# A seven-product scheme for A11 B11 of two row-block pairs, chained in PSUM, in an fp32 relational graph layer

## The chip, the core and the metric

The kernel runs on one NeuronCore of a Trainium2 chip. TensorE (PE) multiplies into PSUM, which has eight banks of 128 partitions x 512 fp32 values; VectorE (DVE) and ScalarE (ACT) read and write PSUM and SBUF; GpSimd (POOL) issues the indirect gathers and scatters; SyncE (SP) issues plain DMAs. Each engine works through its own queue in order, and semaphores tie the queues together. The metric is the device time of one execution in microseconds (us).

## What is computed

Everything is fp32. There are 1250 nodes with 1024 features, 20000 edges and 8 edge types.

```
h = max(layernorm(x), 0)
u = h @ root + bias
for r in range(8):
    mask = (edge_type == r)
    sums = segment_sum(h[src] * mask, dst);  cnt = segment_sum(mask, dst)
    u = u + (sums / max(cnt, 1)) @ weight[r]
z = concat([u, h], 1) @ w_gate + b_gate
out = x + tanh(u) * z + h * (1 - z)
```

The kernel multiplies first and gathers afterwards: it forms h @ weight[r] for every type, h @ root and h @ (lower half of w_gate), ten products of 1250 x 1024 by 1024 x 1024 (matrices s = 0 to 9), gathers rows of them per edge, and ends with u @ (upper half of w_gate).

## The kernel before

**Tiling.** The 1250 rows are ten blocks of 128. Blocks d and d+5 form row-block i = 0 to 4, so each matrix s is five calls of `product`, i = 0 to 4. In a call the left side is a 2 x 2 arrangement of 128 x 512 parts and the right side one of 512 x 512 quarters. `product` computes it with seven products instead of eight (Winograd's form of Strassen): of A11, A12, A22 and sums S1 to S4 on the left, with quarters and sums t1 to t4 on the right. I call such a product a *large* one: `add` (L354) issues four matmuls with a moving operand of 512 columns. Three of the sums live in one PSUM bank `b`: A11, then S2 and then S3 and A22 are added onto it, and between two additions ACT copies the running value out (L395, L402, L380, L429). So each addition to `b` must wait until ACT has read the one before it.

**Inner products.** For s > 0 the rows i = 0, 1 and i = 2, 3 are pairs. The product of A12 with b21 of both rows of a pair is itself done with seven *small* products (class `Second`): `add` (L212) issues two matmuls with 256 columns each. For s > EARLY = 3, that is matrices 4 to 9, the product of S4 with b22 is done so too (class `Third`, its sums in `room`). The small products are put between large ones by hand: `product` calls `filled("first")`, `"fifth"`, `"sixth"`, `"third"`, `"seventh"` and `"fourth"` after the large product of that number, and `step` has a table `fill` of what goes there. `q` is the pair's `Third`, `e` its `Second`. After each large product (and after a fill that returns true) `done()` calls `beside(j)` with j = 0, 1, 2 and so on; there DVE forms the sums, and `between(j)` issues the *slots*: one gather on POOL (L1168) and one DVE multiply-add of 128 x 1024 (L1173) per slot, 1.19 to 1.24 per call for s = 5 to 9.

**The order in matrices 4 to 9** is, by row: i = 0: A11, S1, S2, `e.second`, S3, `q.second`, A22. i = 1: A11, `e.first` (2 small), `q.first` (3), S1, `e.sixth` (2), S2, `e.seventh`, S3, `e.fourth`, `q.last` (3), A22. i = 2: A11, S1, S2, `e.first`, S3, `e.sixth`, `q.second`, `e.seventh`, A22, `e.fourth`. i = 3: A11, `q.first`, S1, S2, `e.second`, S3, `q.last`, A22. i = 4 is alone: A11, S1, S2, S4, S3, A12, A22.

**PSUM.** `bank()` (L121) hands out six banks named `ps`; `ps_n` holds S1 of the first row of a pair until the second (`hold`, L279), `ps_q` is one bank of `Third`. Each `product` takes two of the six for `b` and `c`.

**The end.** After matrix 9, five more calls of `product` multiply u by the upper half of w_gate. In each, `gate_u` transposes two blocks of the next u on PE (`transposed`, L315: four banks, read out alternately by ACT and DVE) after the S4 product, and `gate_rows`, `gate_load` and `finish` put gathers on POOL and elementwise work on DVE.

Of the kernel before, what the change touches and what calls it, by code (L numbers as in the profile page):

```python
# [19 lines left out]
def tile_rgcn_highway(  # L20
# [98 lines left out]
    node_dram = [dram.tile([KEYS, 1], I32, name=f"node_dram{g}") for g in range(G)]  # L119

    def bank():  # L121
        return psum.tile([P, 512], F32, name="ps", bufs=6)


    wbuf = [wpool.tile([P, KQ, Q], F32, name=f"w{i}") for i in range(9)]
# [57 lines left out]
    class Second:  # L183
# [52 lines left out]
        def second(self):  # L236
            self.a = bank()[:, :H]
            self.add(self.a, self.a12, self.b21, True)
# [15 lines left out]
    class Third:  # L254
# [53 lines left out]
        def last_to(self, to, to1, c):  # L308
# [3 lines left out]
                                 to1.rearrange("p (a n) -> p a n", a=2),  # L312
                                 self.b[:, None, :].to_broadcast([P, 2, H]))

    def transposed(aop, part, of, n, relu=False):  # L315


        for half, to in enumerate(((A11, A12), (A21, A22))[part]):
            p = bank().rearrange("p (k f) -> p k f", k=KQ)
            for i in range(KQ):  # L320
                k = KQ * half + i
                nc.tensor.transpose(p[:, i, :n], of[:n, k * P:(k + 1) * P], ident[:n, :n])  # L322
            to_n, p_n = aop[:, to, :, :n], p[:, :, :n]
            if half and relu:
                nc.vector.tensor_scalar_max(to_n, p_n, 0.0)
            elif half:
                nc.vector.tensor_copy(to_n, p_n)
            else:
                nc.scalar.activation(to_n, p_n, AF.Relu if relu else AF.Copy)
            if n < P:  # L330
                nc.gpsimd.memset(aop[:, to, :, n:], 0.0)
# [7 lines left out]
                                                                     aop[:, b])  # L339

    def product(aop, w, to, between=lambda j: None, last=None, pieces=1, whole=True,
                fill=None, second=None, third=None, inner=None):

        c11, c12 = to[0][:, :Q], to[0][:, Q:]  # L350
        c21, c22 = to[1][:, :Q], to[1][:, Q:]
        step = [0]

        def add(b, i, fresh=False, at=slice(0, Q)):  # L354
            for k in range(KQ):
                nc.tensor.matmul(b[:, at], aop[:, i, k, :], w.of[i][:, k, at],  # L356
                                 start=(fresh and k == 0), stop=(k == KQ - 1),
                                 skip_group_check=True)

        def done():  # L360
            between(step[0])
            step[0] += 1

        def filled(name):
            if fill and name in fill and fill[name]():
                done()

        def p3():
            add(c, S4)
            if third:  # L370
                third(c)
            else:
                nc.vector.tensor_add(c12, c12, c)  # L373
            done()
            filled("third")

        def p7():
            d = rows.tile([P, Q], F32, name="part", bufs=2)
            add(b, S3)
            nc.scalar.copy(d, b)  # L380
            nc.vector.tensor_add(c22, c22, d)  # L381
            done()
            filled("seventh")
            return d

        def p2():
            a = bank()
            add(a, A12, True)
            nc.vector.tensor_add(c11, c11, a)
            done()  # L390

        b = bank()
        c = inner.hold() if inner and inner.holds else bank()
        add(b, A11, True)
        nc.scalar.copy(c11, b)  # L395
        done()
        filled("first")
        if second:
            second()
            p2()  # L400
        add(c, S1, True)
        nc.scalar.copy(c22, c)  # L402
        done()
        filled("fifth")
        add(b, S2)
        nc.scalar.copy(c12, b)  # L406
        done()
        filled("sixth")
        if whole and not third:
            p3()  # L410
            d = p7()
            if not second:
                p2()
        else:
            d = p7()
            if third:
                last(d, 0)
            if inner:
                inner.then(c)
                done()  # L420
                filled("third")
            else:
                p3()
        if pieces == 1:
            add(b, A22)
            if last:
                last(b, 0)
            else:
                nc.scalar.copy(c21, b)  # L429
        else:  # L430
            for j in reversed(range(pieces)):
                at = slice(j * Q // pieces, (j + 1) * Q // pieces)
                b = bank()
                add(b, A22, True, at)
                last(b[:, at], at.start, d[:, at])
        done()
        filled("fourth")
# [12 lines left out]
    def thirds(s):  # L450

        return s > EARLY

    waiting, waiting_third = {}, {}

    def step(s, i, between=lambda j: None, second=None):

# [20 lines left out]
            nc.sync.dma_start(to, t[:n])  # L478

        def beside(j):  # L480
            new = fac[s + 1]
            if i == 0 and j == 0 and s > 0:
                fac[s].make_t4()
            if two and i == 0:
                sums(j)
            if q and i % 2 == 0 and j == 1:
                q.sums()
            if q and i % 2 and j == 1:
                q.next_sums()
                q.first_to(to[:, Q:])  # L490
            if q and i % 2 and j == 4:
                q.fifth_to(t[0][:, Q:])
            if two and (i, j) == (1, 6):
                Second(fac[s], 2).left()
            if (s, i, j) == (0, 0, 3) or (s > 0 and (i, j) == (3, 0)):
                new.load_first()
            if (s, i, j) == (0, 0, 3) or (s > 0 and (i, j) == (3, 2)):
                new.load_next()
            if i == NP - 1:
                if j == 0:  # L500
                    new.load_b22()
                elif j == 1:
                    new.make_t1()
                elif j == 3:
                    new.load_b21()
                elif j == 4:
                    new.make_t2()
                elif j == 5:
                    new.make_t3()
            between(j)  # L510

        def sums(j):
# [5 lines left out]
            if j == (0 if s > EARLY else 4):  # L518
                e.left()

        fill = {}
        q = None
        if two:
            e, to = waiting[i - i % 2]
            if thirds(s):
                if i % 2 == 0:
                    waiting_third[i] = Third(fac[s], i, room)
                q = waiting_third[i - i % 2]
                q.holds = i % 2 == 0

                def then(c):
                    if q.holds:
                        q.second(c)
                    else:
                        q.last(c)
                        q.last_to(to[:, Q:], t[0][:, Q:], c)
                        put(i - 1, 0, to)

                q.then = then
            if i == 0:  # L540
                fill = dict(sixth=lambda: (e.second(), e.second_to_first(to)))
            elif i == 1:
                fill = dict(first=lambda: (e.first(), q and q.first(), 0)[-1],
                            fifth=lambda: (e.sixth(), True),
                            sixth=lambda: (e.seventh(), e.to_first(to), 0)[-1],
                            seventh=lambda: (e.fourth(), e.to_second(t[0]),
                                             q or put(i - 1, 0, to), 0)[-1],
                            third=lambda: (e.fourth_to_second(t[0]), 0)[-1])
            elif i == 2:
                fill = dict(sixth=lambda: e.first(),  # L550
                            seventh=lambda: e.sixth(),
                            third=lambda: (e.seventh(), e.to_first(to), 0)[-1],
                            fourth=lambda: (e.fourth(), True))
            else:
                fill = dict(first=lambda: (e.to_second(t[0]), e.fourth_to_second(t[0]),
                                           q and q.first(), 0)[-1],
                            sixth=lambda: (e.second(), True),
                            seventh=lambda: (e.second_to_first(to), q or put(i - 1, 0, to),
                                             0)[-1])
        product(h_op[i], fac[s], t, between=beside, whole=not two, fill=fill, second=second,  # L560
                inner=q)
        for part in range(2):
            if part or not two or i % 2:
                put(i, part, t[part])
# [578 lines left out]
    with ExitStack() as edges_part:  # L1143
# [4 lines left out]
        inner_pool = edges_part.enter_context(tc.tile_pool(name="inner", bufs=1))  # L1148
        room = [inner_pool.tile([P, 2, n], F32, name=f"inner{k}")
                for k, n in enumerate((H, H, P, P))]  # L1150

        fresh = [GOT]

# [87 lines left out]
        def passes_needed():  # L1241
# [7 lines left out]
                                             w_of[:, g, d, K[g][d]:], axis=AX.X)  # L1249
            nc.vector.reduce_max(most[:, 1:2], far_k, axis=AX.X)  # L1250
            for _ in range(30):
                yield
            p = bank()
            nc.tensor.transpose(p[:1, :P], most[:, 0:1], ident)
# [327 lines left out]
```

## Time and profile before

| what | us |
|---|---|
| median of three runs (1352.46 to 1352.57) | 1352.57 |
| the profiled execution | 1355.31 |
| its span, first to last instruction | 1353.5 |
| one matrix, s = 6 to 7 to 8 to 9, start to start | 117.2 |
| DVE busy in 115 us of such a matrix (s = 6, 7) | 86.8 |
| ACT busy in the same | 18.5 |
| from the start of matrix 4 to the end of matrix 9 | about 512 to 1217 |
| one large product, start to start (eight records) | 3.43 |
| one small product, start to start (four records) | 0.86 |
| ACT copy of 128 x 512 / of 128 x 256 | 0.585 / 0.37 |
| DVE addition of 128 x 512 / of 128 x 256, one slot of 128 x 1024 | 0.69 / 0.42, 1.28 |

Of an fp32 matmul the profile has two records. The records' own lengths overlap (a record of 512 columns is 594 ns long, and the next starts 429 ns after it), so what a product costs PE is read from start to start. PE is busy for 99% of the span; DVE has the next largest share, 70%.

### The profile page before, as it was taken

Reading aid. Unit: us, or ns where it says so; the run is one execution under the profiler, and the core shown is the slowest. Engines: PE = TensorE matmul, PEld = TensorE weight load, DVE = VectorE, ACT = ScalarE, POOL = GpSimd, SP = SyncE. Lnnn points to the kernel's source line nnn. Section 1 sums busy time; section 2 is a strip of 40 time slices with the busy share of each in tenths; the row PEclk is TensorE's granted clock in tenths of the full one; section 3 lists DMA queues with packets and bytes.
Section 4 is the critical chain, followed back from the end, with each engine's and each line's share of the span. In section 5 each row is a group of like instructions: output and inputs, shape, how many; then the busy total and the mean of one; then the engine's idle time right before and its main releaser. Section 6 shows DMA issues by size and latency. Waiting matters only on the chain.

```text
span 1353.5 us, 13211 instructions
## 1 busy us (share of the span) xinstructions
PE 1339.7 (99%) x3954; PEld 685.7 (51%) x3954; DVE 942.5 (70%) x1929; ACT 369.9 (27%) x816; POOL 583.2 (43%) x510
## 2 busy tenths in 40 slices
PE   9999999999999999999999999999999999999997
PEld 5444455455445545554554555455455545554443
DVE  6855976786784926335676777877677787677875
ACT  3335656465641111111121111111111111121210
POOL 0001755655553356101444545354445556535641
PEclk9999999999999999999999999999999999999999
DMA  8744675854773162134547778878878967879971
GB/s 307 275 183 148 100 134 144 204 86 124 161 180 83 51 173 48 48 125 160 168 159 277 254 247 316 287 258 295 282 251 288 315 224 209 294 286 275 335 203 58
DMA packets 106909, 271.15 MB, mean 200 GB/s; under 512 B 22693, under 2 KB 24947, under 8 KB 106705
## 3 DMA queue, kind: packets, MB, share of 16 engines
q1 hardware_dynamic: 46640, 120.01, 29.6%
q0 software_dynamic: 44064, 118.28, 27.8%
q10 hardware_dynamic: 16128, 31.98, 7.5%
q8 instruction: 31, 0.51, 0.2%
q14 instruction: 46, 0.37, 0.1%
HBM read 212.71 MB, written 75.66 MB: 213 GB/s over the span
## 4 chain that ended last, share of the span: by engine, by line
PE 90%; issue 4%; DMA 3%; POOL 2%; SPq 0%; ACT 0%; DVE 0%; POOLq 0%; DVEq 0%
PE ps L356 71%; PE ps L214 10%; PE ps_n L356 3%; PE ps_q L214 2%; PE ps_n L214 2%; DMA got<-h_dram,node 1%; DMA w<-in_L_gnn_weight_dram 1%; POOL got L589 1%; POOL out_dram L595 1%; PE ps L322 1%; DMA got<-hr_dram,node 1%; DMA u<-last_dram 1%; PE ps_n L906 1%; POOL w L589 0%; PE ps_q L957 0%
## 5 line engine op out<-in xcount | busy, mean ns | idle before, releaser
L356 PE MATMUL ps<-w,h_op 128*128 128x512 f32 x2512 | 1105.0, 593 | 1.3 <-issue 0.7
L356 PEld LDWEIGHTS ps<-w,h_op 128*128 128x128 f32 x2512 | 471.3, 190 | 542.0 <-issue 527.9
L1168 POOL DMA_INDIRECT got<-y,idx x193 | 251.4, 1303 | 338.4 <-DVE u L1173 202.8
L1173 DVE SCALAR_TENSOR_TENSOR u<-got,w_of,u 128x1024 f32<-128x1024 f32 (+1 forms) x193 | 247.0, 1282 | 80.3 <-DMA got<-y,idx 77.4
L985 POOL DMA_INDIRECT table<-row_col,at_i x157 | 174.7, 1113 | 160.9 <-DVE at_i L981 75.2
L381 DVE TENSOR_TENSOR row<-row,part 128x512 f32<-128x512 f32 x54 | 37.3, 690 | 111.2 <-ACT part L380 105.1
L429 ACT COPY row<-ps 128x512 f32<-128x512 f32 x49 | 28.6, 584 | 212.2 <-PE ps L356 198.5
L380 ACT COPY part<-ps 128x512 f32<-128x512 f32 x55 | 32.2, 585 | 181.2 <-PE ps L356 167.4
L395 ACT COPY row<-ps 128x512 f32<-128x512 f32 x54 | 31.6, 585 | 164.7 <-PE ps L356 149.5
L214 PE MATMUL ps<-w,w 128*128 128x256 f32 x288 | 71.3, 380 | 0.0
L406 ACT COPY row<-ps 128x512 f32<-128x512 f32 x54 | 31.6, 585 | 135.0 <-PE ps L356 131.0
L214 PEld LDWEIGHTS ps<-w,w 128*128 128x128 f32 x288 | 54.3, 190 | 18.4 <-issue 12.0
L911 DVE TENSOR_TENSOR seen<-seen,ps_n 128x100 f32<-128x100 f32 x157 | 40.3, 257 | 27.3 <-PE ps_n L906 11.4
L971 DVE SCALAR_TENSOR_TENSOR junk<-k_bc,key_col,before 128x128 f32<-128x128 int32 x157 | 55.1, 351 | 4.2
L214 PE MATMUL ps<-w,h_op 128*128 128x256 f32 x216 | 56.0, 382 | 0.0
L169 DVE TENSOR_TENSOR w<-w,w 128x2048 f32<-128x2048 f32 (+1 forms) x12 | 25.4, 2113 | 44.0 <-PE ps L356 36.9
L402 ACT COPY row<-ps 128x512 f32<-128x512 f32 x42 | 24.6, 585 | 111.1 <-PE ps L356 105.5
L214 PEld LDWEIGHTS ps<-w,h_op 128*128 128x128 f32 x216 | 40.5, 190 | 25.6 <-issue 21.6
L888 ACT ACTIVATE is_lo<-io,less_lo 128x128 bf16<-128x128 f32 x157 | 50.2, 392 | 0.7 <-DMA xh_dram<-xt 0.7
L626 POOL DMA_INDIRECT node_dram<-ids,pos_i x20 | 28.3, 1416 | 42.8 <-issue 42.8
L373 DVE TENSOR_TENSOR row<-row,ps 128x512 f32<-128x512 f32 x29 | 19.8, 684 | 37.7 <-PE ps L356 25.2
L356 PE MATMUL ps_n<-w,h_op 128*128 128x512 f32 x96 | 43.2, 592 | 0.0
(223 smaller groups left out, 1182.5 us busy)
## 6 DMA issues: line engine op xcount, KB each, us to landing
y<-row SPq DMA_DIRECT2D x72, 512.0 KB
w<-in_L_gnn_weight_dram ACTq DMA_DIRECT2D x21, 1024.0 KB
w<-in_L_gnn_weight_dram SPq DMA_DIRECT2D x10, 1024.0 KB
k_bc<-keys_dram SPq DMA_DIRECT2D x39, 256.0 KB
l_bc<-los_dram SPq DMA_DIRECT2D x39, 256.0 KB
w<-in_L_gnn_w_gate_dram ACTq DMA_DIRECT2D x6, 1024.0 KB
h_dram<-h_op SPq DMA_DIRECT2D x9, 512.0 KB
u<-in_L_gnn_bias_dram SPq DMA_DIRECT2D x9, 512.0 KB
```

The lines of the kernel that those rows point to most:

```text
L214: nc.tensor.matmul(p, a[:, k, :], b[:, k, :], start=(fresh and k == 0), stop=(k == 1), skip_group_check=True)
L356: nc.tensor.matmul(b[:, at], aop[:, i, k, :], w.of[i][:, k, at], start=(fresh and k == 0), stop=(k == KQ - 1), skip_group_check=True)
L380: nc.scalar.copy(d, b)
L381: nc.vector.tensor_add(c22, c22, d)
L395: nc.scalar.copy(c11, b)
L406: nc.scalar.copy(c12, b)
L888: nc.scalar.activation(is_lo[:, i, :], io, AF.Abs, bias=less_lo[:, c0 + i:c0 + i + 1])
L911: nc.vector.tensor_add(seen[j][:, i, :], was, p[:, i, :])
L971: nc.vector.scalar_tensor_tensor(junk, o["k_bc"][:, i, :], key_col[:, c:c + 1], before, op0=OP.is_equal, op1=OP.mult, accum_out=rank[:, c: ...
L985: ins = nc.gpsimd.indirect_dma_start(out=table[:, :], out_offset=bass.IndirectOffsetOnAxis(ap=at_i[:n, i:i + 1], axis=0), in_=row_col[:n, ...
L1168: nc.gpsimd.indirect_dma_start(out=t[:n], out_offset=None, in_=y[g][:, :], in_offset=bass.IndirectOffsetOnAxis(ap=at[:n, d, k:k + 1], axis=0),
L1173: nc.vector.scalar_tensor_tensor(u[:n], t[:n], w, u[:n], op0=OP.mult, op1=OP.add)
```

## The change

For the pairs of matrices 4 to 9, the product A11 B11 of both rows is also done with seven small products (class `First`), and these end up in the PSUM banks in which the rest of the row's chain is then accumulated:

- Two of the `ps` banks become a tag of their own, `ps_b` (`lead()`), for `b`; `bank()` has four.
- `early`, four small products, is put into the `product` call before the pair (i = 4 of the matrix before, or i = 1), ahead of its A22. ACT copies one result from PSUM into half of the new bank `to0` and another to SBUF (`p5_room`); PE adds onto `to0`; DVE writes the other half of `to0` from a sum.
- `late`, three small products, replaces A11 in i = 0 and 2: now S1 is first, then `late`. ACT copies one PSUM half into both halves of `to1`, and PE adds onto `to0` and `to1`. `to0` is then `b` of this row and `to1` is `b` of the next row, which has no A11 product at all; DVE adds `p5` to `to1` (`fifth_to`).
- DVE forms `First`'s sums in `room`, before `early` (`first_sums`) and after it (`next_sums`).
- The fills of these rows are rearranged. The new order is, by row: i = 0: S1, `late` (3), `e.second`, S2, S3, `q.second`, A22. i = 1: `e.first` (2), `q.first` (3), S1, `e.sixth` (2), S2, `e.seventh`, `q.last` (3), `e.fourth`, S3, `early` (4), A22. i = 2: S1, `late`, `e.first`, S2, `q.second`, S3, `e.sixth`, A22, `e.seventh`. i = 3: `e.fourth`, `q.first`, S1, S2, `q.last`, S3, `e.second`, A22. i = 4: A11, S1, S2, S4, S3, A12, `early`, A22.
- The load of the next b11 moves by one call (j = 0 to 1 in i = 3), because `e.fourth` now reads its buffer there. The two transposes of `passes_needed` wait for call 4 of row 4. The store of row i-1 moves with the fills.

```diff
     def bank():
-        return psum.tile([P, 512], F32, name="ps", bufs=6)
+        return psum.tile([P, 512], F32, name="ps", bufs=4)
+    def lead():
+        return psum.tile([P, 512], F32, name="ps_b", bufs=2)
+    class First:
...
+        def early(self):
+            self.to0 = lead()
+            self.x, y = bank()[:, :H], bank()[:, :H]
+            Second.add(self, self.x, self.a11, self.b11, True)
+            nc.scalar.copy(self.to0[:, :H], self.x)
+            Second.add(self, y, self.s1, self.t1, True)
+            nc.scalar.copy(self.p5, y)
+            Second.add(self, self.to0[:, :H], self.a12, self.b21)
+            Second.add(self, self.x, self.s2, self.t2)
+            nc.vector.tensor_add(self.to0[:, H:], self.x, self.p5)
+        def late(self):
+            self.to1 = lead()
+            Second.add(self, self.x, self.s1, self.t1)
+            nc.scalar.copy(self.to1.rearrange("p (a n) -> p a n", a=2),
+                           self.x[:, None, :].to_broadcast([P, 2, H]))
+            Second.add(self, self.to0[:, H:], self.s2, self.b22)
+            Second.add(self, self.to1[:, :H], self.a22, self.t2)
+            return self.to0
+        def fifth_to(self):
+            nc.vector.tensor_add(self.to1[:, H:], self.to1[:, H:], self.p5)
...
+        if first and inner.holds:
+            c = p5()
+            b = p1()
+        else:
+            b = p1()
...
+            if inner and not inner.holds:
+                inner.then(c)
+                done()
+                filled("third")
             d = p7()
...
+        if early:
+            early()
...
             if i == 0:
                 fill = dict(sixth=lambda: (e.second(), e.second_to_first(to)))
+                if q:
+                    fill = dict(first=fill["sixth"], seventh=lambda: (q.second(q.c0), True))
...
+            elif i == 2 and q:
+                fill = dict(first=lambda: e.first(),
+                            sixth=lambda: (q.second(q.c0), True),
+                            seventh=lambda: e.sixth(),
+                            fourth=lambda: (e.seventh(), e.to_first(to), True))
...
+            elif q:
+                fill = dict(first=lambda: (e.fourth(), e.to_second(t[0]),
+                                           e.fourth_to_second(t[0]), q.first(), 0)[-1],
+                            seventh=lambda: (e.second(), True),
+                            fourth=lambda: (e.second_to_first(to), put(i - 1, 0, to), 0)[-1])
```

`First.sums` and `next_sums` are those of `Third` (two additions or subtractions of 128 x 256 and two of 128 x 512 each). In the new `product`, `p1` is A11 (or `late`, or nothing), its copy and `filled("first")`; `p5` is S1, its copy and `filled("fifth")`.

More of the change, by code (lines that the diff above doesn't have):

```diff
@@ L313, in last_to, with __init__, sums, next_sums @@
                                  self.b[:, None, :].to_broadcast([P, 2, H]))
+    class First:
+        def __init__(self, f, i, room, p5):
+            b = f.place["b11"]
+            self.b11, self.b12, self.b21, self.b22 = [
+                b[:, k:k + 2, c:c + H] for k in (0, 2) for c in (0, H)]
+            self.a11, self.a12, self.a21, self.a22 = [
+                h_op[i + o][:, A11, k:k + 2] for o in (0, 1) for k in (0, 2)]
+            self.t1, self.t2, self.s1, self.s2 = room
+            self.p5 = p5
+        def sums(self):
+            Third.sums(self)
+        def next_sums(self):
+            Third.next_sums(self)
+        def early(self):
[18 more added lines that the diff above has]
+            nc.vector.tensor_add(self.to1[:, H:], self.to1[:, H:], self.p5)
     def transposed(aop, part, of, n, relu=False):
@@ L341, in product @@
     def product(aop, w, to, between=lambda j: None, last=None, pieces=1, whole=True,
-                fill=None, second=None, third=None, inner=None):
+                fill=None, second=None, third=None, inner=None, first=None, early=None):
         c11, c12 = to[0][:, :Q], to[0][:, Q:]
@@ L390, in p2, with p1, p5 @@
             done()
[L392 to L404, printed above, removed]
+        def p1():
+            if first is None:
+                b = lead()
+                add(b, A11, True)
+            else:
+                b = first.late() if inner.holds else first.to1
+            nc.scalar.copy(c11, b)
+            done()
+            filled("first")
+            return b
+        def p5():
+            c = inner.hold() if inner and inner.holds else bank()
+            add(c, S1, True)
+            nc.scalar.copy(c22, c)
+            done()
+            filled("fifth")
+            return c
+        if first and inner.holds:
+            c = p5()
+            b = p1()
+        else:
+            b = p1()
+            if second:
+                second()
+                p2()
+            c = p5()
         add(b, S2)
@@ L414, in product @@
         else:
+            if inner and not inner.holds:
+                inner.then(c)
+                done()
+                filled("third")
             d = p7()
@@ L417, in product @@
                 last(d, 0)
[L418 to L422, printed above, removed]
-                p3()
+            if not inner:
+                p3()
+        if early:
+            early()
         if pieces == 1:
@@ L452, in thirds, with next_first @@
         return s > EARLY
-    waiting, waiting_third = {}, {}
+    waiting, waiting_third, waiting_first = {}, {}, {}
+    at_call = [0, 0]
+    def next_first(s, i):
+        if thirds(s) and i == 1:
+            return s, 2
+        if thirds(s + 1) and i == NP - 1 and s + 1 < NM - 1:
+            return s + 1, 0
+        return None
     def step(s, i, between=lambda j: None, second=None):
@@ L480, in beside @@
         def beside(j):
+            at_call[:] = i, j
             new = fac[s + 1]
@@ L485, in beside @@
                 sums(j)
-            if q and i % 2 == 0 and j == 1:
+            if q and i % 2 == 0 and j == 3:
+                waiting_first[s, i].fifth_to()
                 q.sums()
@@ L490, in beside @@
                 q.first_to(to[:, Q:])
-            if q and i % 2 and j == 4:
+            if q and i % 2 and j == 3:
                 q.fifth_to(t[0][:, Q:])
+            if coming and j == (4 if i == 1 else 2):
+                first_sums()
             if two and (i, j) == (1, 6):
                 Second(fac[s], 2).left()
-            if (s, i, j) == (0, 0, 3) or (s > 0 and (i, j) == (3, 0)):
+            if (s, i, j) == (0, 0, 3) or (s > 0 and (i, j) == (3, int(thirds(s)))):
                 new.load_first()
@@ L519, in sums, with first_sums, early @@
                 e.left()
+        coming = next_first(s, i)
+        def first_sums():
+            waiting_first[coming] = First(fac[coming[0]], coming[1], room, p5_room)
+            waiting_first[coming].sums()
+        def early():
+            waiting_first[coming].early()
+            waiting_first[coming].next_sums()
         fill = {}
@@ L531, in then @@
                 def then(c):
[L532 to L537, printed above, removed]
+                    q.last(c)
+                    q.last_to(to[:, Q:], t[0][:, Q:], c)
                 q.then = then
@@ L544, in step @@
                             fifth=lambda: (e.sixth(), True),
[L545 to L548, printed above, removed]
+                            sixth=lambda: (e.seventh(), e.to_first(to), 0)[-1])
+                if q:
+                    fill.update(third=lambda: (e.fourth(), e.to_second(t[0]),
+                                               put(i - 1, 0, to), 0)[-1],
+                                seventh=lambda: (e.fourth_to_second(t[0]), 0)[-1])
+                else:
+                    fill.update(seventh=lambda: (e.fourth(), e.to_second(t[0]),
+                                                 put(i - 1, 0, to), 0)[-1],
+                                third=lambda: (e.fourth_to_second(t[0]), 0)[-1])
+            elif i == 2 and q:
[3 more added lines that the diff above has]
+                            fourth=lambda: (e.seventh(), e.to_first(to), True))
             elif i == 2:
@@ L553, in step @@
                             fourth=lambda: (e.fourth(), True))
-            else:
-                fill = dict(first=lambda: (e.to_second(t[0]), e.fourth_to_second(t[0]),
-                                           q and q.first(), 0)[-1],
+            elif q:
[3 more added lines that the diff above has]
+                            fourth=lambda: (e.second_to_first(to), put(i - 1, 0, to), 0)[-1])
+            else:
+                fill = dict(first=lambda: (e.to_second(t[0]), e.fourth_to_second(t[0]), 0)[-1],
                             sixth=lambda: (e.second(), True),
-                            seventh=lambda: (e.second_to_first(to), q or put(i - 1, 0, to),
-                                             0)[-1])
+                            seventh=lambda: (e.second_to_first(to), put(i - 1, 0, to), 0)[-1])
         product(h_op[i], fac[s], t, between=beside, whole=not two, fill=fill, second=second,
-                inner=q)
+                inner=q, first=waiting_first.get((s, i - i % 2)) if two else None,
+                early=early if coming else None)
         for part in range(2):
@@ L1150, in tile_rgcn_highway @@
                 for k, n in enumerate((H, H, P, P))]
+        p5_room = inner_pool.tile([P, H], F32, name="inner4")
         fresh = [GOT]
@@ L1251, in passes_needed @@
             for _ in range(30):
+                yield
+            while at_call != [NP - 1, 4]:
                 yield
```

## The prediction

> **What bounds the kernel now.** I read the busy times first, then the chain of waits, then PE's timeline.
>
> ```profile
> PE 1339.7 (99%) x3954; PEld 685.7 (51%) x3954; DVE 942.5 (70%) x1929; ACT 369.9 (27%) x816; POOL 583.2 (43%) x510
> PEclk9999999999999999999999999999999999999999
> PE 90%; issue 4%; DMA 3%; POOL 2%; SPq 0%; ACT 0%; DVE 0%; POOLq 0%; DVEq 0%
> ```
>
> PE is busy throughout, at full clock, and 90% of the chain that ended last is PE. A high busy share alone could hide waits, so I read starts in its timeline:
>
> ```profile
> 703.09 1.03 PE L214 MATMUL ps_q<-w,h_op 128*128 128x256 f32 x4
> 703.95 1.03 PE L214 MATMUL ps<-inner,inner 128*128 128x256 f32 x4
> ...
> 750.41 3.60 PE L356 MATMUL ps_n<-w,h_op 128*128 128x512 f32 x8
> 753.84 3.60 PE L356 MATMUL ps<-w,h_op 128*128 128x512 f32 x8
> 757.28 1.03 PE L214 MATMUL ps<-w,h_op 128*128 128x256 f32 x4
> ```
>
> A large product takes 3.43 (750.41 to 753.84), a small one 0.86 (703.09 to 703.95), a quarter as much. Matrix 6 has 27 large and 28 small ones: row by row 5+5+5+5+7 large, 2+12+7+7 small; 27 x 3.433 + 28 x 0.858 = 116.7. Measured, start to start: 117.2. So PE loses only 0.5 per matrix. Here PE is the bound, every microsecond of PE work saved is a microsecond of span, and every new PE wait costs in full.
>
> **What is saved.** Per pair two large products go (6.87) and seven small ones come (6.01): 0.86. Twelve pairs: **-10.3**.
>
> One rule speaks against this. The Trainium skill, "TensorE: Matmul & The Clock Gate", section "Back-to-back issue gap", says that in a stream of weight loads and matmuls both set the spacing, and that at small N the formula from columns alone is too low: about 81 ns against 56 at N = 128, 25 ns more. Halving the columns doubles the weight loads per column. If each of the 12 x 7 x 4 = 336 new records paid 25 ns, 8.4 of the 10.3 would be gone. The row decides: four records take 0.86, exactly a quarter of a large product's 3.43, since the 190 ns weight load still fits under 215 ns. I take no charge.
>
> **New bare waits on ACT.** An addition onto a bank must wait for ACT's copy of what is in it. The trace has this with a small product as cover:
>
> ```profile
> 712.54 1.03 PE L214 MATMUL ps<-w,h_op 128*128 128x256 f32 x4
> 712.74 0.59 ACT L406 COPY row<-ps 128x512 f32<-128x512 f32 x1 [2.80 <-PE ps L356]
> ...
> 713.38 0.30 PEld L356 LDWEIGHTS ps<-w,h_op 128*128 128x128 f32 x2 [0.21 <-ACT row L406]
> 713.41 2.82 PE L356 MATMUL ps<-w,h_op 128*128 128x512 f32 x6
> ```
>
> S2's stream ends at 712.54, when the cover starts. ACT copies from 712.74 to 713.33; the weight load that waited for it starts at 713.38, and that S3 takes 3.51 in the chain instead of 3.43. So a copy of 512 columns needs 0.86 + 0.08 = 0.94 of cover; a copy of 256 needs 0.94 - 0.585 + 0.37 = 0.73. Then I go through the new order for additions to one bank with nothing between:
> - i = 0, S2 then S3: the fill "sixth" is gone. Bare: 0.94 x 6 matrices = **+5.7**.
> - `e.seventh` (end of i = 2), then `e.fourth` (start of i = 3), both on `e.b`, with the copy to p7 between them; before, the large A22 lay there. 0.73 x 6 = **+4.4**.
> - One small product as cover (0.08 lost): four places per matrix before (i = 0 twice, i = 1, i = 3); five after (both `late`s, i = 0 S3, i = 2 S2, i = 3 S3). **+0.5**.
> - Elsewhere at least two small products or a large one lie between. In `early`, the half copy needs 0.73 and has 0.86.
>
> ACT's copies from PSUM to PSUM have no row. I take 0.37 and 0.585; the ends are 0 and twice the row. ACT has 18.5 of 115 busy, but a doubled 512 copy in `late` would add 12 x 0.6 = 7, a free one would give back 1.
>
> So the saving is used up by its own waits: -10.3 + 5.7 + 4.4 + 0.5 = **+0.3**.
>
> **DVE.** Each pair adds two sets of sums (2.2 each) and two additions of 0.42: 5.3, 63 in all. DVE has
>
> ```profile
> 749.00:864.00 115.00, 115.00 (x324) 61.03 (x323) 86.80 (x104) 18.52 (x36) 57.54 (x47) 1.00 0.80 278
> ```
>
> 86.8 busy of 115 (third column of engines); 10.6 more per matrix still fits, so DVE is no bound on average. But PE now waits for it at a place with little slack: `early` in i = 1 needs s1 and t1 from `first_sums`, which stand in DVE's queue behind `q.last_to`, and that behind the queue of i = 1:
>
> ```profile
> 788.03 0.68 DVE L381 TENSOR_TENSOR row<-row,part 128x512 f32<-128x512 f32 x1
> 788.63 0.41 DVE L306 TENSOR_TENSOR row<-row,ps 128x256 f32<-128x256 f32 x1
> 788.96 2.60 DVE L1173 SCALAR_TENSOR_TENSOR u<-got,w_of,u 128x1024 f32<-128x1024 f32 x2
> 791.47 0.42 DVE L248 TENSOR_TENSOR row<-row,w 128x256 f32<-128x256 f32 x1
> 791.93 0.42 DVE L249 TENSOR_TENSOR row<-row,w 128x256 f32<-128x256 f32 x1
> 792.27 0.68 DVE L309 TENSOR_TENSOR row<-row,ps_n 128x512 f32<-128x512 f32 x1
> ```
>
> `q.last_to` (L309) starts at 792.27 though PE finished `q.last` at 790.21: DVE is 2 late there. In the new order L381, the two slots of call 4 and L248/L249 fall behind it: 0.69 + 2.6 + 0.84 = 4.1 earlier, 788.1. I add 1 for backlog from the new sums (ends 0 and 3: before this place DVE spends about 8 waiting for gathers in this matrix, which swallow some of it): 789.1. Then L309 to L311 2.04, s1 0.42, t1 0.69: ready at 792.3. PE: S3 of i = 1 starts at 783.24; in its place come `q.last` 2.58, `e.fourth` 0.86, S3 3.43, the first product of `early` 0.86: needed at 791.0. Wait 1.4. The same sum with L309's other starts (674.63, 909.02, 1024.89, 1143.54) and one slot in call 4 gives 2.2, 2.3, 0.9, 2.4; none in matrix 4, which has no slots. Together **+9** (backlog 0: 4; backlog 3: 19). Behind this wait PE's whole queue stands. `next_sums` for `late` comes out 1 to 3 ahead of need; `q.last`, moved up, needs the older `next_sums` at 783.24 in i = 1, and L277 ends at 782.1: 1 of slack. I charge both nothing; with backlog 3 they add about 5.
>
> **Banks.** With four `ps` instead of six. In the program as built before, a new tile almost always takes the buffer let go earliest (225 of 241 times); I take that rule. Then in matrices 4 to 9 `x` gets `q.c`'s bank, free since call 3. At the end the fourth transposed half of each product gets `c`'s bank, whose last reader is DVE's L373 just before. Its slacks are 0.35, 0.36, -3.2, 0.14, -0.1; the bad one:
>
> ```profile
> 1257.01 1.91 PE L322 MATMUL ps<-ident,u 128*128 128x128 f32 x16
> 1259.72 1.23 DVE L1386 TENSOR_TENSOR u<-u,got 128x1024 f32<-128x1024 f32 x1 [1.95 <-DMA got<-hr_dram,node]
> 1260.87 0.68 DVE L373 TENSOR_TENSOR row<-row,ps 128x512 f32<-128x512 f32 x1
> ```
>
> The fourth half starts at 1258.32, L373 ends at 1261.55: 3.2 plus 0.15 of signal, and 0.3 for the last: **+3.7** (ends 0 and 7). At the start one S1 (68.5) waits 0.2.
>
> **Moved steps.** The store of row i-1 goes to SP later in i = 3 (after A22 instead of before); its `row` buffer is next written by ACT 6.9 into i = 4, which covers a store; without cover up to 2 per matrix. Nothing queued behind it on SP is awaited by PE soon. The b11 load moves some 6 later on ACT's queue, behind `e.fourth`; its reader comes 20 later. POOL issues the same gathers, held back as DVE frees buffers. Two transposes move (0.22 of PE). All at 0.
>
> **Sum.** -10.3 + 5.7 + 4.4 + 0.5 + 9 + 3.7 = +13. The profiled execution, 1355.3 (span 1353.5 and 1.8 around it), would be 1368; the median shown lies 2.7 lower, so 1352.6 + 13 = 1365.5. I say **1365**.
>
> **Rivals.**
> 1. *DVE keeps up.* The gather waits swallow all the new DVE work and the transposes find their bank free: +0.3 to +2, 1353 to 1355. For it: 28 us of DVE idle per matrix. Against: L309 was late in five matrices of six already. 0.12.
> 2. *The bare waits are shorter and the saving shows.* At S2 to S3 of i = 0 and `e.seventh` to `e.fourth`, if only the copies' own 0.585 and 0.37 count (drain and signal hidden), they cost 5.7 and not 10.1: with rival 1, -4, **1348.5**. It decides once both waits together stay under 1.2 per matrix. Against: 712.54 to 713.38 shows drain and signal in full. 0.04.
> 3. *DVE sets the pace of the pairs.* Backlog 3 and more: waits also at `late` and `q.last`, +19 +5 + 4 = +28, 1380. For it: DVE goes to 97 of 115, and its waits for gathers (DMA share 0.80) don't all shrink. 0.13.
> 4. *Banks go in fixed turn.* Then `x` waits for L252, the last DVE step before `early`: about 5 per matrix in place of 1.5, 1352.6 + 0.3 + 3.7 + 30 = 1387. 0.03.
>
> My forecast has 0.68, with 1357 to 1373 its own range. The range over all, 1354 to 1380, leaves out rivals 2 and 4 and parts of 1 and 3. Differences under 0.2% (2.7 us) can't be told from none here: faster is rival 2, 0.04; within is rival 1 and the low end of mine, 0.12; slower 0.84.
>
> **What would show it.** In the new profile: a PE gap of 0.9 before S3 of row 0 and 0.7 before `e.fourth`, six times each; PE waiting on DVE's inner sums before the second small product of `early`; a PE wait of 3 on L373 at the third set of final transposes; matrices 5 to 9 about 118 to 119 apart instead of 117.2. A spacing of 117.2 refutes the DVE step; one near 115.5 refutes the bare waits.

## The result, and the profile after

The change makes the kernel slower: 1363.55 us median (1361.2 to 1365.16) against 1352.57 for the kernel before, ratio 1.0075 with a 95% interval of 1.0056 to 1.0094. Measured a second time (e5 below): 1363.5, ratio 1.007 [1.0051, 1.0089]. The profiled execution of after took 1361.2 (span 1359.4) and lies at the low end of the runs shown; that of before, at 1355.31, lay at their high end. So the two traces differ by 5.9 us of span, the medians by 11.

The busy times of after (engine, us, share of the span, instructions):

```profile
PE 1336.1 (98%) x4098; PEld 712.2 (52%) x4098; DVE 995.2 (73%) x2049; ACT 384.1 (28%) x852; POOL 592.6 (44%) x510
```

PE's busy time falls by 3.6 us and the span grows by 5.9: PE now waits. The view of PE's waits says for whom (instruction that waits, what it waits for: us in total, times, longest):

```profile
PE ps_b L403 <- ACT row L468: 4.1, 6, 0.7
PE ps L403 <- ACT row L453: 3.0, 1, 3.0
PE ps L218 <- ACT w L235: 2.8, 6, 0.5
PE ps L369 <- DVE row L420: 1.5, 1, 1.5
PE ps L671 <- POOL eps L673: 1.4, 1, 1.4
PE ps L218 <- DVE inner L273: 1.2, 1, 1.2
```

Only L671 (L572 in that kernel) was there before; two waits of the kernel before, 2.7 in all for an ACT cast (L941) ahead of matrix 4, did not come in this execution, which is one more part of why the spans differ by less than the medians. The others are the prediction's places: L468 is S2's copy in row 0, L235 the copy after `e.seventh`, L273 the sum t1 that `early` reads, L420 the reader of `c` before the transposes. L453 is the store's, which the prediction had put at nothing.

**The two bare waits** in the timeline (start, us, engine, line, operation, instructions, idle before and its releaser), first S2 to S3, then `e.seventh` to `e.fourth`, in matrix 6:

```profile
757.85 0.58 ACT L468 COPY row<-ps_b 128x512 f32<-128x512 f32 x1 [4.69 <-PE ps_b L403]
...
758.49 1.98 PE L403 MATMUL ps_b<-w,h_op 128*128 128x512 f32 x4 [0.68 <-ACT row L468]
...
816.30 1.03 PE L218 MATMUL ps<-w,w 128*128 128x256 f32 x4
...
817.79 1.13 PE L218 MATMUL ps<-w,h_op 128*128 128x256 f32 x4 [0.46 <-ACT w L235]
```

The idle column (0.68, 0.46) understates them, since PE's records overlap. From start to start, `e.seventh` to `e.fourth` takes 1.49 instead of 0.86, and the product that waited is itself 0.10 longer: 0.73. The same reading gives 0.94 at S2 to S3 (4.27 from start to start instead of 3.43, and 0.10). Each comes six times: 5.65 and 4.4.

**The store's wait**, matrix 8, row 4:

```profile
1077.47 1.72 SPq L551 DMA_DIRECT2D hr_dram<-row  x3
...
1080.41 3.60 PE L403 MATMUL ps_b<-w,h_op 128*128 128x512 f32 x8
...
1086.38 0.58 ACT L453 COPY row<-ps 128x512 f32<-128x512 f32 x1 [8.57 <-DMA hr_dram<-row]
...
1087.02 5.40 PE L403 MATMUL ps<-w,h_op 128*128 128x512 f32 x8 [3.01 <-ACT row L453]
```

The first of the three issues is the store of row 2's results, at 1077.47; the other two are row 3's own. ACT's copy of S1 wants to write the `row` buffer that this store still reads, and gets it 8.9 later, at 1086.38. PE's next addition to that bank, S4, waits for the copy. In before, the same store and the same copy are these:

```profile
1073.78 0.32 SPq L478 DMA_DIRECT2D hr_dram<-row  x1
...
1081.59 0.58 ACT L402 COPY row<-ps 128x512 f32<-128x512 f32 x1 [2.80 <-PE ps L356]
```

That copy came 7.8 after the issue and waited for PE alone. In after the issue comes late even for its new place: A22 of row 3 had ended by 1073.75, when ACT copied it, but the store must wait for the last addition to row 2's results (L249), and DVE came to that only after three slots that had waited for gathers:

```profile
1077.04 0.41 DVE L249 TENSOR_TENSOR row<-row,ps 128x256 f32<-128x256 f32 x1
```

The wait has a tail: the eight records after it span 5.40 us, not 3.60. The windows show why (stretch, then its length and busy us of PE, PEld, DVE, ACT, POOL, then the clock granted to PE, the DMA share, GB/s):

```profile
1087.00:1088.00 1.00, 0.98 (x3) 0.51 (x4) 0.26 (x1) 0.45 (x1) 0.00 (x0) 1.00 1.05 426
1088.00:1089.00 1.00, 1.00 (x3) 0.51 (x2) 1.00 (x1) 0.00 (x0) 0.00 (x0) 0.66 1.02 416
1089.00:1090.00 1.00, 1.00 (x2) 0.33 (x1) 0.02 (x1) 0.00 (x0) 0.71 (x1) 0.50 1.01 412
```

The clock is halved from about 1088.3 to 1091.7. Wait and slow records together put this stretch 4.9 us behind the usual pace. While the store was under way, the DMA share was 0.79 and 0.76 in the two stretches of 2 us from 1078 on, and 1.0 at some 420 GB/s from 1082 on, so full DMA engines are at most a part of why it took 8.9.

**`early` waiting for DVE** is there once, in matrix 6:

```profile
786.34 0.68 DVE L313 TENSOR_TENSOR row<-row,ps_n 128x512 f32<-128x512 f32 x1
...
787.06 1.03 PE L218 MATMUL ps<-w,h_op 128*128 128x256 f32 x4
...
788.59 0.68 DVE L273 TENSOR_TENSOR inner<-w 128x512 f32<-128x512 f32 x1
...
789.33 1.13 PE L218 MATMUL ps<-inner,inner 128*128 128x256 f32 x4 [1.24 <-DVE inner L273]
```

PE ended `q.last` near 782.7 and DVE's `last_to` (L313) starts 3.6 later, so t1 (L273) ends at 789.27, 1.36 after PE wanted it. By matrix, start to start (us):

| matrix | 4 | 5 | 6 | 7 | 8 |
|---|---|---|---|---|---|
| before | 117.2 | 117.4 | 117.2 | 117.2 | 117.2 |
| after | 117.4 | 117.6 | 119.1 | 117.4 | 122.3 |
| after, second measurement (e5) | 117.4 | 117.6 | 118.5 | 117.4 | 124.5 |

In matrices 4, 5 and 7 the saving and the bare waits just cancel.

### The profile page after: what moved, and what is told of

Read it like the earlier page. It is cut to its first block, busy times and chain, and to the rows that moved or that the text cites. A ratio compares the mean times of both kernels' runs of the same rounds, so it can differ in the third digit from the quotient of the medians.

```text
span 1359.4 us, 13672 instructions
## 1 busy us (share of the span) xinstructions
PE 1336.1 (98%) x4098; PEld 712.2 (52%) x4098; DVE 995.2 (73%) x2049; ACT 384.1 (28%) x852; POOL 592.6 (44%) x510
## 5 line engine op out<-in xcount | busy, mean ns | idle before, releaser
L403 PE MATMUL ps_b<-w,h_op 128*128 128x512 f32 x1560 | 702.1, 595 | 5.0 <-ACT row L468 4.1
L403 PEld LDWEIGHTS ps_b<-w,h_op 128*128 128x128 f32 x1560 | 291.6, 190 | 334.5 <-issue 316.9
L1268 POOL DMA_INDIRECT got<-y,idx x193 | 261.6, 1355 | 335.8 <-DVE u L1273 206.0
L403 PE MATMUL ps<-w,h_op 128*128 128x512 f32 (+1 forms) x760 | 340.3, 591 | 3.0 <-ACT row L453 3.0
L1273 DVE SCALAR_TENSOR_TENSOR u<-got,w_of,u 128x1024 f32<-128x1024 f32 (+1 forms) x193 | 246.9, 1282 | 54.1 <-DMA got<-y,idx 47.3
L403 PEld LDWEIGHTS ps<-w,h_op 128*128 128x128 f32 x760 | 143.8, 191 | 167.7 <-issue 161.2
L427 ACT COPY part<-ps_b 128x512 f32<-128x512 f32 x55 | 32.2, 585 | 218.2 <-PE ps_b L403 218.2
L428 DVE TENSOR_TENSOR row<-row,part 128x512 f32<-128x512 f32 x54 | 37.2, 689 | 70.2 <-ACT part L427 70.2
L493 ACT COPY row<-ps_b 128x512 f32<-128x512 f32 x49 | 28.6, 584 | 185.8 <-PE ps_b L403 185.8
L468 ACT COPY row<-ps_b 128x512 f32<-128x512 f32 x54 | 31.6, 585 | 146.0 <-PE ps_b L403 145.9
L218 PE MATMUL ps<-w,h_op 128*128 128x256 f32 x264 | 69.0, 384 | 2.8 <-ACT w L235 2.8
L218 PEld LDWEIGHTS ps<-w,h_op 128*128 128x128 f32 x264 | 49.1, 190 | 26.6 <-issue 16.1
L453 ACT COPY row<-ps 128x512 f32<-128x512 f32 x42 | 24.6, 585 | 120.1 <-PE ps L403 104.4
L445 ACT COPY row<-ps_b 128x512 f32<-128x512 f32 x54 | 31.7, 587 | 89.8 <-PE ps_b L403 83.7
L218 PE MATMUL ps<-inner,inner 128*128 128x256 f32 x192 | 49.4, 380 | 1.2 <-DVE inner L273 1.2
L420 DVE TENSOR_TENSOR row<-row,ps 128x512 f32<-128x512 f32 x29 | 19.8, 684 | 41.9 <-PE ps L403 30.7
```

The costliest lines, as they stand in the source:

```text
L218: nc.tensor.matmul(p, a[:, k, :], b[:, k, :], start=(fresh and k == 0), stop=(k == 1), skip_group_check=True)
L1268: nc.gpsimd.indirect_dma_start(out=t[:n], out_offset=None, in_=y[g][:, :], in_offset=bass.IndirectOffsetOnAxis(ap=at[:n, d, k:k + 1], axis=0),
L1273: nc.vector.scalar_tensor_tensor(u[:n], t[:n], w, u[:n], op0=OP.mult, op1=OP.add)
```

## The experiments

The kernels ran in four groups (e1 to e4, e5 to e8, e9 to e11, e12), each with runs of the kernel before on the same chip, whose medians were 1355.72, 1352.76, 1352.89 and 1352.51. So ratios are compared; 0.001 is 1.35 us. The theory to be tested was the prediction's: each wait costs its own length, so each comes back when its cause is taken away. The main rival, which the spread of the change's runs suggests: a wait that is removed lets PE come sooner to the next one (the store's, or DVE's), and little comes back.

### Each bare wait covered alone, the banks alone, the sums alone

**e1**: `e.second` back between S2 and S3 of row 0.

```diff
-                    fill = dict(first=fill["sixth"], seventh=lambda: (q.second(q.c0), True))
+                    fill.update(seventh=lambda: (q.second(q.c0), True))
```

> In row 0 of matrices 4 to 9, e.second goes back between S2 and S3. Theory (bare waits on ACT): the wait before S3 of row 0, 0.94 us in each of six matrices in the profile of the change, shrinks to the 0.1 that one small product leaves, and late's own second and third product still cover the copy of A11 before S2: 5.0 us less than the change's 1363.6, so 1358.5. Rival (the rows behind the pair are paced by DVE or by stores, and PE would wait there for what it doesn't wait for here): at most 1 us less, 1362.5 or more, with the saved time coming back as waits on DVE.

Measured 1360.95, ratio 1.004 [1.0023, 1.0057]: some 4.5 less than the change (1.007 to 1.0075), near the 5.0 expected, with an uncertainty of 3.4. In its list of PE's waits, L468 is gone, and the wait for t1 has grown:

```profile
PE ps L218 <- DVE inner L273: 4.1, 2, 2.9
PE ps L369 <- DVE row L420: 3.2, 1, 3.2
```

**e2**: `q.first` between `e.seventh` and `e.fourth`.

```diff
-                fill = dict(first=lambda: (e.fourth(), e.to_second(t[0]),
-                                           e.fourth_to_second(t[0]), q.first(), 0)[-1],
+                fill = dict(first=lambda: (q.first(), e.fourth(), e.to_second(t[0]),
+                                           e.fourth_to_second(t[0]), 0)[-1],
```

> In row 3 of matrices 4 to 9, q.first's three small products go ahead of e.fourth. Theory (bare waits): the 0.73 us before e.fourth goes in six matrices, 4.4 us less than 1363.6: 1359.2. Rival (paced elsewhere): at most 1 us less.

Measured 1363.57, 1.0065 [1.004, 1.009]. The bare wait left the trace, but the run shown by the profile lost 4.5 at the store. By itself it decides nothing: the interval holds both the full gain and none.

**e3**: the kernel before with only the change's bank tags (four `ps`, two `ps_b`) and its moved transposes.

> The kernel before, with only its PSUM banks split as in the change (four ps, two for b). Theory: the fourth transposed half of the last five products now takes the bank of c and waits for DVE's L373 once: 1.7 (as in the profile of the change) to 3.7 (as predicted) over 1352.6, so 1354.3 to 1356.3, with a PE wait on DVE near the third set of final transposes. Rival (the banks cost nothing and the change's wait there comes from its busier DVE): 1352.6, no such wait.

Measured 1359.06, 1.0025 [1.0013, 1.0038]: 3.3 of cost by the ratio. Its trace has the third set of transposes waiting 3.0 for the reader of `c` (L376 in that kernel), as the prediction had it, and then PE's clock halved. This was the slowest of its 22 runs (1368.42): it lost as much again, 3.0 and a slow clock, where S1 of row 2 in matrix 9 waited for DVE to read `ps_n`, a bank outside the split:

```profile
PE ps L325 <- DVE row L376: 3.0, 1, 3.0
PE ps_n L359 <- DVE row L312: 3.0, 1, 3.0
```

**e4**: the change without `First`'s sums, but for the first pair; the small products read what is in `room`, and nothing else moves.

```diff
-            waiting_first[coming].sums()
+            if coming == (EARLY + 1, 0):
+                waiting_first[coming].sums()
```

and `next_sums` in the same way.

> The change with the sums of First (sums and next_sums) left out for every pair but the first, so the small products of A11 B11 use what lies in the buffers; about 49 us of DVE work go, PE's work stays. Theory of the prediction (PE waits on DVE for these sums in early, 9 us in all): 1354.5. Theory from the one profile of the change (it waits there in one matrix of six, 1.5 us; the rest of the time is in the bare waits and in a store that row 4 waits for): 1359 to 1362. Rival (DVE plays no part): 1363.6.

Measured 1362.52, 1.0056 [1.0037, 1.0074]: 2 to 2.5 below the change, which isn't told apart from nothing. The 9 us that the prediction gave to DVE's sums did not come back. By the intervals it was some 6 at the most. So the sums themselves were not the main part of what the change lost.

### The covers together, then the store, then the bank

**e5** is the change again, beside the others on that chip.

> The change as it is, beside the kernel before on the same chip, as the mark for the others. 8 to 11 us over the kernel before in these rounds (11 in its first result; e1, e2 and e4, each with one part eased, stood 5 to 8 over theirs). Its trace should show the two bare waits six times each at 0.94 and 0.73 again, and other waits (inner sums, a store, the transposes) at different places or lengths than in the first trace, since they hang on when DMAs land.

Measured 1363.5 (1358 to 1366.93), 1.007 [1.0051, 1.0089]. Its trace has both bare waits six times, and one of 4.9 for the store.

**e6** joins e1 and e2.

> Both bare waits covered: e.second between S2 and S3 in row 0, q.first ahead of e.fourth in row 3. Theory (bare waits 10.0 us, gain of seven products 10.3 us): 9.4 us below the change, so 1 us below to 2 us above the kernel before. Rival (PE is paced by DVE and stores behind the pairs): 1 to 4 us below the change, still 5 or more above the kernel before, with longer waits on DVE's inner sums.

Measured 1360.04, 1.0062 [1.004, 1.0084]: 1 us under e5 by the ratio, 3.5 by the medians, 5 at the most by the interval. The 9.4 are not there, though both bare waits are gone. Its PE waits, longest first:

```profile
PE ps L403 <- ACT row L453: 8.4, 2, 4.6
PE ps L369 <- DVE row L420: 1.7, 1, 1.7
...
PE ps L218 <- DVE inner L273: 1.3, 1, 1.3
```

The store's wait is now there in matrices 7 and 8; after and e5 have it in 8 alone. In matrix 7 PE starts S1 of row 4 6.4 earlier than in after (953.17 for 959.61), but DVE comes to the store's last addition, and so the store is issued, only 3.9 earlier (955.18 for 959.07). So the time that PE had lost before was, in part at least, cover for this wait; that the store also took 8.2 to free its buffer, where in after's matrix 7 the copy found it free 4.2 after the issue, is not explained by the order. Each wait meets a stretch at half clock: records that span 3.60 otherwise span 5.25 and 5.40.

**e7** keeps both covers and gives the store back its place: the addition that reads `e.second` of row 3 goes, with the store, between S3 and A22.

```diff
-                            seventh=lambda: (e.second(), True),
-                            fourth=lambda: (e.second_to_first(to), put(i - 1, 0, to), 0)[-1])
+                            seventh=lambda: (e.second(), e.second_to_first(to),
+                                             put(i - 1, 0, to), True))
```

> Both covers, and in row 3 the last addition to the row of row 2 and its store go ahead of A22 instead of behind it. Theory (row 4's ACT copy of S1 waits for that store's buffer, 3.2 us in matrix 8 in the first trace, and the PE clock falls behind it): no such wait in the trace, 1 to 4 us below both covers alone. Rival (the store is late because DMA is busy, not because it is issued late): same as both covers alone within 1 us.

Measured 1356.72, 1.0032 [1.0021, 1.0043], about 4 under e6 (0.0030, uncertain by 0.0025). No wait for L453 is left, and what had stood behind it is now first: 5.5 for L273 in three places, 2.5 for L279 (`next_sums`).

**e8** takes e7, and gives the fourth half of the final transposes a `ps_b` bank (`transposed(..., last=lead)`).

> As the one before, and the fourth transposed half of the last five products takes a bank of ps_b, whose last reader is one product back, instead of the bank of c. Theory (with banks alone costing 3.3 us, most of it at the third set of transposes): no PE wait there, 2 to 4 us below e7 and 2 to 5 below the kernel before. Rival (DVE's copy of that half is late anyway and PE waits for it at the next left sums): within 1 us of e7.

Measured 1355.15, 1.0013 [1.0004, 1.0022], 2.6 under e7 (uncertain by 1.9), but still over the kernel before, where 2 to 5 below it was expected. **e11** is e3 with this mend.

> The kernel before with the split banks of e3 and the mend of e8 (the fourth transposed half takes a bank of ps_b). Theory (e3's 3.3 us are that wait and the slow clock behind it): 0 to 1 us over the kernel before, and no PE wait at the third set of transposes. Rival (four banks also cost elsewhere, in the first four matrices or at S1): 2 to 3 us over it as in e3.

Measured 1353.92, 1.0006 [0.9998, 1.0015]. So the split of the banks cost 3.3, and with the transposes mended 0.8 (between -0.3 and 2.0). The difference, 2.6, is uncertain by 2.1, and agrees with the 2.6 from e7 to e8.

### What DVE's sums cost once all else is covered

**e9** is e8 with `early` put ahead of A12 in row 4 and `e.first` of row 2 ahead of `late`: more distance from the sums to `late`.

> As e8, and DVE's sums get more time before PE needs them: in row 4 early goes ahead of the A12 product instead of behind it (3.4 us more for the sums that late needs), and in row 2 e.first goes ahead of late (1.7 us more). Theory (what is left over e8's best run is PE waiting on DVE's sums in matrices 8 and 9, at late by 3 us and at early by 3 to 4): the wait at late goes, the one at early in row 1 stays; 1 to 3 us below e8's place (2.4 over the kernel before), so 1 below to 2 above it. Rival (DVE's backlog moves on with the sums): the wait shows at the next place, same as e8.

Measured 1356.26, 1.0024 [1.0014, 1.0033]: no gain. `late`'s wait (2.9 in e8) went, and the one at `early` in matrix 9 grew:

```profile
1135.73 1.03 PE L218 MATMUL ps<-w,h_op 128*128 128x256 f32 x4
1142.23 2.07 PE L218 MATMUL ps<-inner,inner 128*128 128x256 f32 x4 [5.48 <-DVE inner L273]
```

Between these two DVE waited 2.07 for a gather, took two slots and the five additions of `to_first` and `last_to`, and only then came to L272 and L273. A wait of 1.2 for the store (L453) is back too.

**e10** is e8 without `First`'s sums, but for the first pair, as in e4.

> As e8, with First's sums left out for every pair but the first (its small products use what lies in the buffers). If what is left between the saving and the result is PE waiting on these sums, this shows the full gain: 10.3 saved, some 1.3 lost at the twelve lates and 0.5 elsewhere, so 8 to 9 below the kernel before in the undisturbed runs, and no PE wait on the inner sums in the trace. Rival (the waits come from gathers and DMA, whatever DVE has to do): within 3 us of e8.

Measured 1344.62 (1344.21 to 1345.96), 0.9939 [0.9925, 0.9953]: 8.3 under before, and matrices of 115.8 to 116.0. Its longest waits of PE:

```profile
PE ps L369 <- DVE h_op L798: 1.5, 1, 1.5
PE ps L673 <- POOL eps L675: 1.4, 1, 1.4
```

None is for an inner sum. So 8.3 of the 10.3 saved are there, and the same sums that were worth 2 in the change (uncertain by 3.6) are worth 10 here (1.0013 to 0.9939, uncertain by 2.3).

**e12** is e8 with `First` left out in matrix 9, where row 1's `early` had the least slack; two of the twelve pairs keep A11 as a large product.

```diff
-        if thirds(s + 1) and i == NP - 1 and s + 1 < NM - 1:
+        if thirds(s + 1) and i == NP - 1 and s + 1 < NM - 2:
```

and the like for row 1, with `e.to_second` and the store after `third` and `e.fourth` after `seventh` there.

> As e8, but in matrix 9 the product A11 B11 stays two large products (with the fills that fit, e.fourth between S3 and A22 of row 1): PE has 1.7 us more work, DVE 10.6 us less in the matrix whose gathers are latest. Theory (e8's remaining loss over its 8.3 us gain without sums is PE waiting on DVE's sums, nearly all in matrix 9 in three traces): the waits go with their cause, 4 to 7 below the kernel before, 1346 to 1349 beside 1352.9. Rival (DVE's work matters wherever it is, and the wait moves to matrix 8): 1 below to 3 above the kernel before.

Measured 1348.17 (1346.87 to 1350.71), 0.9965 [0.9953, 0.9977]: faster than before by 4.7, and than the change by 14 to 15. One wait for a sum is left in its trace, 1.6 in matrix 6.

## Why the prediction was right, and where its steps were not

The time (1365 said, 1363.55 measured) and the direction were right. The sum behind it was right in the terms that PE's own order sets, and wrong in three that depend on other queues; their errors have opposite signs, and that the number came so close is in part luck.

| step | said | in after's trace, or by a run |
|---|---|---|
| seven small for two large products | -10.3 | -8.3 with covers and without sums (e10) |
| S2 to S3, row 0 | +5.7 | +5.65 |
| `e.seventh` to `e.fourth` | +4.4 | +4.4 |
| one small product as cover | 0.08 each | 0.08 or 0.105 each |
| `early` waiting for the sums | +9 | +1.5 (e5: 0.8 of idle time) |
| the bank of the fourth half | +3.7 | +1.7; +3.3 alone, slow clock included (e3) |
| the store, moved | 0 | +4.9 |

With the trace's values in place of the prediction's, and the saving at 10.3, the sum is, by estimate, about +8.5. The two traces differ by 5.9, or by 8.6 without the 2.7 that only before lost ahead of matrix 4, so the list is near complete for this execution. The prediction said +13, the medians +11: DVE and the bank came to 3.2 where 12.7 was said, and 4.9 came from a step priced at nothing. e5's trace is of an execution near the median (1363.29): it is 2.1 longer than after's, and so is its matrix 8, where the store's wait is.

**The saving and the bare waits.** The row outweighed the rule on small N: e10's matrices take 115.8 to 116.0, near the 115.5 that the counts give, so small products cost a quarter of a large one; e10 still bears the single covers and what is left of the banks, by estimate 1 to 2 together. Both bare waits came out to a tenth, since they were built from a case in the trace with drain and signal in it, and not from the copy's 0.585. Rival 2 falls with that. A small doubt named there is settled too: ACT's copies from PSUM to PSUM in `early` and `late` take 0.36 and 0.57, like any other.

**The DVE step failed**, in its size: +9, of which 1.5 came. The wait was said for matrices 5 to 9 and came in 6 alone; by the prediction's own test (a spacing of 117.2) it is refuted in 5 and 7. The wrong term is the backlog at `last_to`: it took the start of L309 in before, subtracted the work that moves behind it, and held the rest to be DVE's backlog. In matrix 5, these lines of before's timeline stand ahead of L309's start at 674.63:

```profile
664.98 0.42 DVE L242 TENSOR_TENSOR row<-row,ps 128x256 f32<-128x256 f32 x1
670.38 0.69 DVE L381 TENSOR_TENSOR row<-row,part 128x512 f32<-128x512 f32 x1 [4.98 <-ACT part L380]
```

DVE was not late there: it stood idle for 4.98 us, waiting for the copy of S3, and L381 is one of the instructions that move behind `last_to`. Its idle time moves with it. In matrix 8 the same idle time is 3.82, but in 7 only 0.97 and in 9 none, so there it explains little or nothing. Measured in after, `last_to` starts 0, 0, 3.6, 0.7, 1.2 and 1.9 after the end of `q.last` in matrices 4 to 9; the prediction had 4.2, 3.3, 4.2, 2.9 and 4.3 for 5 to 9. Only matrix 6, the one whose lines were shown (no idle time in them), was right: 1.4 said, 1.36 measured. What else covered the sums: DVE's busy time grew by 52.7 (the prediction's 63 adds record lengths that overlap), while its waits for gathers fell from 77.4 to 47.3 and those for S3's copy from 105.1 to 70.2. So most of the new work went into time that DVE had idled; which of it helped in 7 and 9 was not taken apart.

**The store failed**, as a step priced at nothing. The prediction followed the right chain (`row` buffer, ACT, PE) and judged 6.9 us enough for a store, counted from the end of A22. But the store waits for DVE too, and was issued some 3.7 after A22's copy; then it took 8.9 to free the buffer. By estimate, issued at 1073.75 and with the same 8.9, it would have been done at 1082.7 and cost PE nothing. Its fallback, "up to 2 per matrix", was short as well: it held no slow clock. e6 against e7 shows the cause, since only the store and the addition ahead of it move between them.

**The banks** were right in place and mechanism. After's trace has 1.7 where e3 measured 3.3: how late the reader of `c` is differs by execution. In e3's trace, as in before's, DVE had just waited for gathers (0.76 and 1.32); in after's it had not.

**What the steps left out** is that such waits don't add. PE's delays before a pinch are cover at the pinch. So the bare waits hid waits for the store and the sums, and the store hid sums: removing 10 us of bare waits brought 1 to 3.5 (e6; at most 5, and e1's 4.5 for one of them lies within the noise of that), and the sums that cost 2 in the change cost 10 in e8. The prediction added its terms as if independent; for its total this made little odds. Rival 1 was right that DVE keeps up in most matrices, and wrong that the kernel would then end at 1353 to 1355. Rival 3 did not occur in this kernel. Rival 4, banks in fixed turn, has no trace: no wait on L252's bank appears.

Left open: why the store takes 8.9 to free its buffer in matrix 8 of after, and 9.4 in e5, where e7's store there took 4.9. In after the DMA engines were full for part of that time, and no run changed that traffic.

## What to carry to other kernels

A start that is late in a trace is not a backlog: look for the idle time in it, and ask whether what it waited for moves too. Sum the waits only where none can hide another; with PE the bound, a bare wait is worth less than its length while another stands behind it, and the gain of a fix may show only when the next wait in the same pinch is mended too. A store moved later is a wait on the next writer of its buffer; count its slack from when the engine that writes the row last gets there, not from its place in the program.

## What the hardware showed

A PE stop of some 3 us costs more than itself. In these traces every stop of 2.85 us or more met a granted clock of one half, for 3.4 us or for twice that; the stops of up to 2.55 us met none.

| half clock for | stops of PE (us) |
|---|---|
| 0 | all up to 2.0; 2.55 (e7) |
| 3.4 | 2.85 (e1), 2.9 (e8), 3.0 (after), 3.5 (e7), 3.8 and 4.6 (e6), 4.9 (e5) |
| 6.8 | 3.0 twice (e3), 3.2 (e1), 4.5 (e2), 5.5 (e9) |

In after the clock fell 1.3 us after PE had resumed, and four records came 0.85 apart instead of 0.43: 1.8 us on top. In e3 it had fallen 0.7 to 0.8 before PE resumed, and the next large product spanned 6.18 and 6.66 instead of 3.60. The Trainium skill, "TensorE: Matmul & The Clock Gate", section "What's actually happening", has half clock after an idle window of about 3.4 us and full clock after a busy one of as much; the lengths seen here, 3.4 and 6.8, are one and two such windows, and a stop of 2.85 was already enough. So a wait of 3 is to be priced at about 5 to 6.5.
